# Four tiles to a round in an attention layer: a Trainium2 kernel of four graph layers

## The chip, the cores and the metric

The kernel runs on one NeuronCore of a Trainium2 chip. Five engines work side by side, each through its own list of instructions in order: PE (TensorE, matrix products; the loading of its weights is listed apart as PEld), DVE (VectorE), ACT (ScalarE), POOL (GpSimd) and SP (which only issues DMAs). An instruction waits until what it depends on is done, and whatever is behind it on its engine waits with it. Products land in PSUM, which ACT and DVE can read and write; everything else lies in SBUF. The metric is the device time of one execution in microseconds (us). The kernel before took 625.76 us, the median of 3 runs (624.59 to 626.89).

## What is computed

The input is `x` (4096 x 64) and a 0/1 adjacency matrix `adj` (4096 x 4096, one entry in about a thousand set). Four layers are applied, each to the normalised rows of `x`, each added to `x`. Layer 0 is the one that matters here:

```python
h = jnp.maximum(_layernorm(x, axis=-1), 0.0)
# in layer 0:
h = lorentz_linear(x, W, b, scale)
q = lorentz_linear(h, Wq, bq, scale_q)
k = lorentz_linear(h, Wk, bk, scale_k)
qm = jnp.concatenate([-q[:, :1], q[:, 1:]], axis=-1)
att = 2.0 + 2.0 * (qm @ k.T)
att = jax.nn.sigmoid(att / att_scale + att_bias)
att = adj * att
support = att @ h
inner = -support[:, :1] ** 2 + jnp.sum(support[:, 1:] ** 2, axis=-1, keepdims=True)
denorm = jnp.sqrt(jnp.clip(jnp.abs(-inner), 1e-08, None))
return support / denorm
```

So a full 4096 x 4096 matrix of scores is formed, passed through a sigmoid, masked by `adj` and multiplied by `h`, all in float32. Layers 1 to 3 use `adj` again: as weights by rank of the neighbour, as a plain sum, and as a mean over neighbours.

## The kernel before

**Tiles.** The output rows are cut into 8 blocks of 512 (`IB`), the neighbours into 16 groups of 256 (`NG` groups of `CG` = 2 times 128). A tile is one block by one group: 128 partitions x 1024 numbers. Layer 0 has 8 x 16 = 128 tiles. For each tile

- PE forms the scores: four records of `scores` (line 908), a product with 64 rows that uses the upper and the lower half of the array at once;
- ACT takes the sigmoid, from PSUM back into the same PSUM (`sigmoids`, line 914);
- DVE multiplies by the mask and writes `att` in SBUF (`masked`, line 927), which sets the PSUM buffer free;
- PE gathers: `gather` (line 935) adds the tile's product with `fb` (the rows h) to the block's sum, with 64 columns, the left and the right half of the array at once.

**Rounds.** In the main loop of layer 0 (from line 1024) PE is given the scores of a round of tiles, then the gathers of the round before, then the next scores. The sizes of the rounds are written out: 3, 3, 3, 3, 2, 2 for a block's 16 tiles. Three PSUM buffers hold scores (two of pool `pp`, one of `spare`), taken in turn, so tile n needs what tile n-3 had. Four buffers (`ATTS`) hold `att`.

**Beside each tile** the loop issues one load of a mask (POOL, line 176: float32 in HBM, 8-bit in SBUF), on ten tiles of sixteen one check that half a tile of `adj` is 0 or 1 (`check`, line 351: SP loads 256 KB into one of three buffers, DVE reads them), and one step of the jobs in hand (`step`). A job is the end of a block (`rows0`): PE transposes its sum (line 229, in `turned`), POOL, ACT and DVE normalise it and make layer 1's features `h` from it, which are written into `fa` and split by `split` into two half-precision parts in `s2a`. Six tiles after a block's first gather, the queries of the next block are transposed on PE from `fa` (line 846) and laid out by ACT (line 856).

**The first block** is done otherwise. Its tiles, the first two of the next block and the whole preparation of h, q and k go as parts with a duration each into `Listing`: `plan` takes at each step the part that can begin first, with places (PSUM and `att` buffers) that a part takes and another frees; `run` tries 2,500 random shifts of the parts' ranks and emits the best plan found. While it runs, `spare` does not exist yet, so two PSUM buffers hold scores.

**Memory.** `fa` holds first the queries, then the features of layer 1, then those of later layers. When layer 0 is done its pools are closed, and `s2b` and the buffers `ckw` of the later, larger checks take their memory.

Of the kernel before, what the change touches and what calls it, by code (L numbers as in the profile page):

```python
# [11 lines left out]
F32 = mybir.dt.float32  # L12
BF16 = mybir.dt.bfloat16
FP8 = mybir.dt.float8e4
FP16 = mybir.dt.float16
# [33 lines left out]
def kernel(  # L49
# [84 lines left out]
    def model(general):  # L134
# [10 lines left out]
        ROWS = ((16, 16), (0, 16))  # L145
        main = pool("main", 1)
        x_sb = main.tile([P, NT, D], F32, name="x_sb" + sfx)
        fa = main.tile([P, NT, D], F32, name="fa" + sfx)
        rdegs = main.tile([P, NT], F32, name="rdegs" + sfx)

        def rows_in(gr):
# [27 lines left out]

        EARLY = 4  # L180
        CHECKED = 3
        ATTS = 2 if general else 4
        parts = pool("parts", 1)
        s2a = parts.tile([P, NT, 2, D], FP16, name="s2a" + sfx)
        epi = pool("epi", 1)
        pm = pool("pm", 1, space=PSUM)
        mp0 = pool("mask_a", 1, side="right")
# [75 lines left out]

        def norm(rows, h, tag, table, up=UP):

            xr = x_sb[:, rows, :]
            st = small("st", tag)
            nc.vector.tensor_reduce(st, xr, AX.X, ALU.add)
            nc.vector.tensor_scalar(st, st, -1.0 / D, None, ALU.mult)  # L269
            yield  # L270
            xc = rows_tile("xc", tag)
            nc.gpsimd.tensor_tensor(xc, xr, bc(st, CI), ALU.add)  # L272
            yield
            sq = rows_tile("sq", tag)
            nc.scalar.activation(sq, xc, AF.Square)
            yield
            va = small("va", tag)
            nc.vector.tensor_reduce(va, sq, AX.X, ALU.add)
            if table:
                yield  # L280
                rs = small("rs", tag)
                nc.scalar.activation(
                    rs, va, AF.Sqrt, bias=eps if up == 1.0 else eps_up, scale=1.0 / D / up / up
                )
                yield
                nc.vector.reciprocal(rs, rs)
            else:
                nc.vector.tensor_scalar(va, va, 1.0 / D / up / up, EPS / up / up, ALU.mult, ALU.add)
                rs = rsqrt(va, tag)
                yield  # L290
                yield
                yield
            nc.vector.scalar_tensor_tensor(h, xc, 0.0, bc(rs, CI), ALU.max, ALU.mult)
            yield

        jobs = deque()

# [96 lines left out]
        class Listing:  # L394
# [3 lines left out]

            HOP, TRIALS = 0.15, 2500

            def __init__(self):
                self.parts = []

            def add(self, engine, us, emit, *after, takes=(), frees=None, at=0.0):
                part = SimpleNamespace(
                    engine=engine, us=us, emit=emit, after=after, takes=takes, frees=frees, at=at,
                    n=len(self.parts), then=[], place=None,
                )  # L410
                for q in after:
                    q.then.append(part)
                self.parts.append(part)
                return part

            def plan(self, names, lead):

                busy, places = {}, dict.fromkeys(names, 0.0)
                at = [part.at for part in self.parts]
                open_ = [len(part.after) for part in self.parts]  # L420
                able = [part for part in self.parts if not part.after]
                where, order, last = {}, [], 0.0
                while able:
                    best = None
                    for part in able:
                        t, place = max(at[part.n], busy.get(part.engine, 0.0)), None
                        if part.takes:
                            free = [(places[n], n) for n in part.takes if places[n] is not None]
                            if not free:
                                continue  # L430
# [8 lines left out]
                    end = busy[part.engine] = t + part.us  # L439
                    last = max(last, end)  # L440
# [46 lines left out]
        def before0(todo, gr, bias):  # L487
# [284 lines left out]
            def qk_rows(u, j, engine):  # L772
                def emit(_):
# [4 lines left out]
                    to = v.kr[:, of(u), :] if j else fa[:, rows(u), :]  # L778
# [7 lines left out]
            def qk_times(u, j):  # L786
                def emit(_):
                    part = slice(u * 2 * HR, (u + 1) * 2 * HR)
                    to = v.kr[:, of(u), :] if j else fa[:, rows(u), :]
# [52 lines left out]
        def queries_turned(ib, pt):  # L842

            for k in range(CI // 2):
                c = ib * CI + 2 * k
                nc.tensor.transpose(
                    pt[:, k, :], fa[:, c : c + 2, :].rearrange("p c d -> p (c d)"), ident
                )

        def queries_laid(ib, pt):  # L850
# [18 lines left out]
        def rows0(ib, asb):  # L869
# [20 lines left out]
            yield  # L890
            yield
            yield
            h = fa[:, rows, :]
            yield from norm(rows, h, tag, False)
            yield from split(h, s2a, rows)
            ready.setdefault(1, set()).add(ib)

# [12 lines left out]
                )  # L910
            return ps

        def sigmoids(ps):
            nc.scalar.activation(ps, ps, AF.Sigmoid, bias=att_c, scale=att_a)  # L914

        def masked(ib, g, ps):

            att = work.tile(
                [P, CG, IB], F32, tag="att", name=f"att_{ib}_{g}{sfx}", bufs=ATTS
            )  # L920
            mask = masks[ib][:, g * CG : (g + 1) * CG, :]
            if general:
                at = load(stream0, ib, g, "at0")
                nc.vector.tensor_tensor(att, ps, at, ALU.mult)
                nc.vector.tensor_scalar(mask, at, 0.0, None, ALU.not_equal, saturate=False)
            else:
                nc.vector.tensor_tensor(att, ps, mask, ALU.mult)  # L927
            return att

        def gather(acc, lhs, g, rhs, at):  # L930

# [8 lines left out]
        def first_rows_and_block():  # L940
# [33 lines left out]
            for n, (ib, g) in enumerate(todo[: NG + 2]):  # L974
# [6 lines left out]
                def emit_scores(_, tile=tile):  # L981
                    tile.ps = scores(tile.ib, tile.g)

                def emit_masked(_, tile=tile):
                    tile.att = masked(tile.ib, tile.g, tile.ps)
                    v.att.append((tile.ib, tile.g, tile.att))

                def emit_gather(_, tile=tile):
                    gather(v.acc, fb, tile.g, tile.att, v.at)
                    v.at += 1  # L990

                sc = add(
                    "PE", 1.0, emit_scores, ktd[u], asked[ib], *(scored if begun else ()),
                    takes=("pp0", "pp1"),
                )
                sg = add("ACT", 1.2, lambda _, tile=tile: sigmoids(tile.ps), sc)
                mu = add(
                    "DVE", 1.25, emit_masked, sg, *(spread if begun else ()), frees=sc,
                    takes=slots,
                )  # L1000
                if begun:
                    continue
                scored.append(sc)
                spread.append(mu)
                add("PE", 1.0, emit_gather, mu, hw[u], room, frees=mu)
            listing.run(("pm", "pa", "ps", "pp0", "pp1", *slots))
            return v.acc, v.att[-2:]

        with tc.manual_schedule():
            acc, late = first_rows_and_block()  # L1010
# [13 lines left out]

            sizes = [2] * 8 if general else [3, 3, 3, 3, 2, 2]
            sizes = sizes[:-1] + (NIB - 2) * sizes + [0]
            k, done = NG + 2, NG
            for size in sizes:  # L1030
                now = []
                for ib, g in todo[k : k + size]:
                    ps = scores(ib, g)
                    sigmoids(ps)
                    now.append((ib, g, masked(ib, g, ps)))
                    load_masks(1)
                    k += 1
                    if k % 8 in (0, 2, 4, 5, 7):
# [18 lines left out]


        s2b = None
        if not general:  # L1060
            s2b = pool("parts_b", 1).tile([P, NT, 2, D], FP16, name="s2b")
            more[:] = pool("ck2", 1), 4
        evac = pool("evac", 1)
        l1 = ExitStack()
# [475 lines left out]
```

## Time and profile before

The profiled execution took 628.15 us by the clock outside, of which its span is 626.3 us. What follows is of that span.

| stage | from, us | to, us | length, us |
|---|---|---|---|
| preparation | 0 | 59.23 | 59.2 |
| rest of the first block, in the planned order | 59.23 | 94.85 | 35.6 |
| main loop of layer 0 | 94.85 | 317.06 | 222.2 |
| layers 1 to 3 | 317.06 | 626.3 | 309.2 |

| a tile of layer 0 | engine | mean ns |
|---|---|---|
| sigmoid, line 914 | ACT | 1175 |
| mask, line 927 | DVE | 1220 |
| check of half a tile, line 351 | DVE | 722 |
| issue of a mask's load, line 176 | POOL | 559 |

The first table comes from the start times of PE's instructions, the second from the groups by line. PE's own records overlap one another (each matmul starts before the one before it has drained), so its pace is read from the distance of starts, not from durations.

### The profile page before, as it was taken

To read this page: it belongs to the slowest core of one execution; us is meant where nothing else is said; L and a number is where in the kernel's file an instruction comes from. 1 tells how busy PE (TensorE), PEld (TensorE's weight loads), DVE (VectorE), ACT (ScalarE), POOL (GpSimd) and SP (SyncE) were. 2 spreads that over 40 slices of the span, in tenths; PEclk is the share of its full clock that TensorE was granted. 3 is DMA by queue.
4 is the path that set the end of the run, shared out by engine and by line. 5 is a ranking of instruction groups with operands and counts; after the bars stand their busy time and mean duration, and the time that the engine had idled before them with its cause. 6 is when DMAs were issued, how large, how long until landed. Compare 5 with 4: busy or idle time off the path is not lost.

```text
span 626.3 us, 9053 instructions
## 1 busy us (share of the span) xinstructions
PE 573.7 (92%) x3012; PEld 232.0 (37%) x3012; DVE 483.8 (77%) x951; ACT 337.1 (54%) x541; POOL 225.4 (36%) x459
## 2 busy tenths in 40 slices
PE   0776999999999999999998999999999999998995
PEld 0653223333333333333343344343443544444542
DVE  5768567998888888888968767768666669988853
ACT  1467567666667676666624676767665014431220
POOL 7423301565656564733336300100000314543152
PEclk9996999999999999999998999999998999999998
DMA  8991924699999898982276342333434375558921
GB/s 138 141 103 12 104 23 77 99 153 140 160 144 158 141 151 144 141 154 84 85 255 194 125 135 100 105 131 102 130 107 134 131 255 189 173 181 291 326 101 40
DMA packets 43880, 87.03 MB, mean 139 GB/s; under 512 B 5232, under 2 KB 22256, under 8 KB 43824
## 3 DMA queue, kind: packets, MB, share of 16 engines
q1 hardware_dynamic: 24672, 68.53, 33.3%
q0 software_dynamic: 18720, 17.57, 30.3%
q8 instruction: 25, 0.41, 0.3%
q10 hardware_dynamic: 432, 0.26, 0.2%
q14 instruction: 31, 0.25, 0.1%
HBM read 135.63 MB, written 1.05 MB: 218 GB/s over the span
## 4 chain that ended last, share of the span: by engine, by line
PE 67%; DVE 14%; DMA 6%; POOL 4%; issue 4%; ACT 4%; SPq 0%; DVEq 0%; POOLq 0%; ACTq 0%
PE ps L908 15%; PE acc L935 14%; PE acc L1293 10%; PE acc L1223 9%; PE cnt L1185 9%; DVE ckw L351 4%; PE cnt L1195 3%; DVE att L927 3%; DMA ckw<-adjt_dram 3%; DMA mask<-adjt_dram 2%; ACT ps L914 2%; PE pt L229 1%; DMA x_sb<-x_dram 1%; PE ps_h L615 1%; PE pr L1099 1%
## 5 line engine op out<-in xcount | busy, mean ns | idle before, releaser
L914 ACT ACTIVATE ps<-ps,att_c,att_a 128x1024 f32<-128x1024 f32 x128 | 146.9, 1175 | 82.7 <-PE ps L908 82.6
L927 DVE TENSOR_TENSOR att<-ps,mask 128x1024 f32<-128x1024 f32 x128 | 155.1, 1220 | 39.0 <-ACT ps L914 38.2
L908 PE MATMUL ps<-qt,kt 64*128 64x512 f32 x512 | 133.6, 630 | 5.2 <-DVE att L927 4.3
L351 DVE SCALAR_TENSOR_TENSOR ckw<-ckw 128x1024 f32<-128x1024 f32 x93 | 119.5, 1298 | 8.0 <-DMA ckw<-adjt_dram 8.0
L935 PE MATMUL acc<-att,fb 128*64 128x512 f32 x512 | 123.1, 607 | 0.7 <-DVE att L927 0.7
L1211 ACT ACTIVATE w<-cnt 128x512 int16<-128x512 f32 x176 | 93.1, 597 | 49.1 <-PE cnt L1195 48.8
L1209 DVE TENSOR_SCALAR w<-cnt 128x512 int16<-128x512 f32 x80 | 53.7, 688 | 38.0 <-PE cnt L1195 37.2
L176 POOL DMA_DIRECT2D mask<-adjt_dram x128 | 70.1, 559 | 20.4 <-DMA mask<-adjt_dram 18.6
L908 PEld LDWEIGHTS ps<-qt,kt 64*128 64x128 f32 x512 | 44.0, 187 | 87.5 <-DVE att L927 41.1
L1185 PE MATMUL cnt<-mask,after 128*128 128x512 fp8e4 x256 | 67.6, 385 | 4.7 <-DVE w L1209 4.3
L1223 PE MATMUL acc<-w,s2a 128*128 128x512 bf16 x256 | 67.8, 387 | 0.1
L935 PEld LDWEIGHTS acc<-att,fb 128*64 128x64 f32 x512 | 31.8, 136 | 81.1 <-issue 76.6
L272 POOL TENSOR_TENSOR xc<-x_sb,st 128x256 f32<-128x256 f32 x24 | 19.0, 793 | 110.0 <-DVE st L269 69.1
L1293 PE MATMUL acc<-mask,s2a 128*128 128x512 fp8e4 x256 | 57.8, 379 | 0.0
L1293 PE MATMUL acc<-mask,s2b 128*128 128x512 fp8e4 x256 | 57.7, 379 | 0.0
L351 DVE SCALAR_TENSOR_TENSOR ck<-ck 128x512 f32<-128x512 f32 x70 | 50.5, 722 | 0.0
L258 POOL TENSOR_TENSOR rs_a<-rs_y 128x4 f32<-128x4 f32 x48 | 17.3, 360 | 89.4 <-DVE rs_y L254 81.2
L1185 PEld LDWEIGHTS <-after 128*128 128x128 bf16 x256 | 25.1, 100 | 34.5 <-issue 7.7
L1293 PEld LDWEIGHTS <-s2b 128*128 128x128 f16 x256 | 25.0, 98 | 27.6 <-issue 0.8
L1293 PEld LDWEIGHTS <-s2a 128*128 128x128 f16 x256 | 24.7, 98 | 27.3
L1223 PEld LDWEIGHTS <-s2a 128*128 128x128 f16 x256 | 20.0, 98 | 30.7 <-issue 15.6
L213 ACT ACTIVATE asb<-acc,level 128x512 f32<-128x512 f32 x23 | 15.4, 692 | 28.3 <-PE acc L1293 28.3
(192 smaller groups left out, 531.9 us busy)
## 6 DMA issues: line engine op xcount, KB each, us to landing
ckw<-adjt_dram SPq DMA_DIRECT2D x93, 512.0 KB, 4.1
ck<-adjt_dram SPq DMA_DIRECT2D x70, 256.0 KB, 5.8
mask<-adjt_dram POOLq DMA_DIRECT2D x128, 128.0 KB, 9.4
x_sb<-x_dram SPq DMA_DIRECT2D x4, 256.0 KB, 8.2
out_dram<-y POOLq DMA_DIRECT2D x6, 128.0 KB, 2.2
w_sb<-wts_dram SPq DMA_DIRECT2D x2, 80.0 KB, 7.9
vec<-vecs_dram ACTq DMA_DIRECT2D x1, 130.5 KB, 6.1
out_dram<-y SPq DMA_DIRECT2D x1, 128.0 KB, 1.9
```

Of the source, the lines that this page charges most:

```text
L176: nc.gpsimd.dma_start(out=masks[ib][:, g * CG : (g + 1) * CG, :], in_=adjt[ib, g])
L272: nc.gpsimd.tensor_tensor(xc, xr, bc(st, CI), ALU.add)
L351: nc.vector.scalar_tensor_tensor(at, at, 0.0, at, ALU.not_equal, ALU.not_equal, accum_out=odd[:, k : k + 1])
L908: nc.tensor.matmul(ps[:, c, :], kt[half, g, :], qts[ib][half, :], start=True, stop=True)
L914: nc.scalar.activation(ps, ps, AF.Sigmoid, bias=att_c, scale=att_a)
L927: nc.vector.tensor_tensor(att, ps, mask, ALU.mult)
L935: nc.tensor.matmul(acc[c * D : (c + 1) * D, :], lhs[:, t, :], rhs[:, c, :], start=(at == 0), stop=(at == NG - 1), skip_group_check=True,)
L1185: nc.tensor.matmul(cnt, after, masks[ib][:, t, :], start=True, stop=True, skip_group_check=True)
L1209: nc.vector.tensor_scalar(w, cnt, 0.0, None, ALU.max)
L1211: nc.scalar.activation(w, cnt, AF.Relu)
L1223: nc.tensor.matmul(accs[ib], both(s2a, t), w, start=(t == NT - 1), stop=False, skip_group_check=True,)
L1293: nc.tensor.matmul(acc, both(s2, t), masks[ib][:, t, :], start=(t == 0), stop=(t == NT - 1), skip_group_check=True,)
```

## The change

- **Rounds of four.** The main loop's rounds become 4, 4, 3, 3 for the rest of the second block and 4, 4, 4, 4 for every later one. There are still three PSUM buffers.
- **The first of a round is masked in SBUF.** In a round of four, the first tile's sigmoid is written by ACT into its `att` buffer in SBUF, and DVE multiplies there in place. Its PSUM buffer is free after the sigmoid. In the planned first block this holds for all 18 tiles.
- **Six `att` buffers** in place of four.
- **Queries share memory with `s2a`.** `q_sb` is the memory of `s2a` read as float32. `fa` is made only after layer 0, and the job's `h` of layer 1 stays in `xc`.
- **The plan counts changes of mode.** Scores and gathers get a `form`; `plan` adds `TURN` = 0.12 us where an engine's form changes, and scores and gathers count 0.88 us in place of 1.0. A score's PSUM place is freed by the sigmoid, and the `att` place is taken by the sigmoid.

```diff
-        fa = main.tile([P, NT, D], F32, name="fa" + sfx)
...
-        ATTS = 2 if general else 4
+        ATTS = 2 if general else 6
         parts = pool("parts", 1)
         s2a = parts.tile([P, NT, 2, D], FP16, name="s2a" + sfx)
+        q_sb = s2a.rearrange("p t k d -> p t (k d)").bitcast(F32)
...
+            h = xc if h is None else h
             nc.vector.scalar_tensor_tensor(h, xc, 0.0, bc(rs, CI), ALU.max, ALU.mult)
...
-            HOP, TRIALS = 0.15, 2500
+            HOP, TURN, TRIALS = 0.15, 0.12, 2500
...
-                        t, place = max(at[part.n], busy.get(part.engine, 0.0)), None
+                        free_at = busy.get(part.engine, 0.0)
+                        if forms.get(part.engine) != part.form:
+                            free_at += self.TURN
+                        t, place = max(at[part.n], free_at), None
...
-            h = fa[:, rows, :]
-            yield from norm(rows, h, tag, False)
+            h = yield from norm(rows, None, tag, False)
...
-        def sigmoids(ps):
-            nc.scalar.activation(ps, ps, AF.Sigmoid, bias=att_c, scale=att_a)
+        def sigmoids(ps, to=None):
+            to = ps if to is None else to
+            nc.scalar.activation(to, ps, AF.Sigmoid, bias=att_c, scale=att_a)
+            return to
...
-                nc.vector.tensor_tensor(att, ps, mask, ALU.mult)
+                nc.vector.tensor_tensor(att, frm, mask, ALU.mult)
...
                 sc = add(
-                    "PE", 1.0, emit_scores, ktd[u], asked[ib], *(scored if begun else ()),
-                    takes=("pp0", "pp1"),
+                    "PE", 0.88, emit_scores, ktd[u], asked[ib], *(scored if begun else ()),
+                    takes=("pp0", "pp1"), form="scores",
                 )
-                sg = add("ACT", 1.2, lambda _, tile=tile: sigmoids(tile.ps), sc)
-                mu = add(
-                    "DVE", 1.25, emit_masked, sg, *(spread if begun else ()), frees=sc,
+                sg = add(
+                    "ACT", 1.2, emit_sigmoids, sc, *(spread if begun else ()), frees=sc,
                     takes=slots,
                 )
+                mu = add("DVE", 1.25, emit_masked, sg)
...
-            sizes = [2] * 8 if general else [3, 3, 3, 3, 2, 2]
-            sizes = sizes[:-1] + (NIB - 2) * sizes + [0]
+            sizes = [2] * 8 if general else [4] * 4
+            first = [2] * 7 if general else [4, 4, 3, 3]
+            sizes = first + (NIB - 2) * sizes + [0]
...
-                    sigmoids(ps)
-                    now.append((ib, g, masked(ib, g, ps)))
+                    if size == 4 and not now:
+                        att = frm = sigmoids(ps, att_tile(ib, g))
+                    else:
+                        frm, att = sigmoids(ps), att_tile(ib, g)
+                    masked(ib, g, frm, att)
+                    now.append((ib, g, att))
...
+        parts_b = pool("parts_b", 1)
+        fa = parts_b.tile([P, NT, D], F32, name="fa" + sfx)
         if not general:
-            s2b = pool("parts_b", 1).tile([P, NT, 2, D], FP16, name="s2b")
+            s2b = parts_b.tile([P, NT, 2, D], FP16, name="s2b")
             more[:] = pool("ck2", 1), 4
```

More of the change, by code (lines that the diff above doesn't have):

```diff
@@ L292, in norm @@
                 yield
+            h = xc if h is None else h
             nc.vector.scalar_tensor_tensor(h, xc, 0.0, bc(rs, CI), ALU.max, ALU.mult)
             yield
+            return h
         jobs = deque()
@@ L394, in model, with add @@
         class Listing:
-            HOP, TRIALS = 0.15, 2500
+            HOP, TURN, TRIALS = 0.15, 0.12, 2500
             def __init__(self):
                 self.parts = []
-            def add(self, engine, us, emit, *after, takes=(), frees=None, at=0.0):
+            def add(self, engine, us, emit, *after, takes=(), frees=None, at=0.0, form=None):
                 part = SimpleNamespace(
                     engine=engine, us=us, emit=emit, after=after, takes=takes, frees=frees, at=at,
-                    n=len(self.parts), then=[], place=None,
+                    form=form, n=len(self.parts), then=[], place=None,
                 )
@@ L416, in plan @@
             def plan(self, names, lead):
-                busy, places = {}, dict.fromkeys(names, 0.0)
+                busy, forms, places = {}, {}, dict.fromkeys(names, 0.0)
                 at = [part.at for part in self.parts]
@@ L439, in plan @@
                     end = busy[part.engine] = t + part.us
+                    forms[part.engine] = part.form
                     last = max(last, end)
@@ L777, in emit @@
                     r3 = v.rrq[:, part].rearrange("p (s k j) -> p s k j", s=2, j=2)[:, :, :, j]
-                    to = v.kr[:, of(u), :] if j else fa[:, rows(u), :]
+                    to = v.kr[:, of(u), :] if j else q_sb[:, rows(u), :]
                     engine.tensor_tensor(
@@ L788, in emit @@
                     part = slice(u * 2 * HR, (u + 1) * 2 * HR)
-                    to = v.kr[:, of(u), :] if j else fa[:, rows(u), :]
+                    to = v.kr[:, of(u), :] if j else q_sb[:, rows(u), :]
                     nc.scalar.mul(
@@ L846, in queries_turned @@
                 nc.tensor.transpose(
-                    pt[:, k, :], fa[:, c : c + 2, :].rearrange("p c d -> p (c d)"), ident
+                    pt[:, k, :], q_sb[:, c : c + 2, :].rearrange("p c d -> p (c d)"), ident
                 )
@@ L911, in scores, with att_tile, masked @@
             return ps
-        def sigmoids(ps):
-            nc.scalar.activation(ps, ps, AF.Sigmoid, bias=att_c, scale=att_a)
-        def masked(ib, g, ps):
-            att = work.tile(
+        def att_tile(ib, g):
+            return work.tile(
                 [P, CG, IB], F32, tag="att", name=f"att_{ib}_{g}{sfx}", bufs=ATTS
             )
+        def sigmoids(ps, to=None):
+            to = ps if to is None else to
+            nc.scalar.activation(to, ps, AF.Sigmoid, bias=att_c, scale=att_a)
+            return to
+        def masked(ib, g, frm, att):
             mask = masks[ib][:, g * CG : (g + 1) * CG, :]
@@ L923, in masked @@
                 at = load(stream0, ib, g, "at0")
-                nc.vector.tensor_tensor(att, ps, at, ALU.mult)
+                nc.vector.tensor_tensor(att, frm, at, ALU.mult)
                 nc.vector.tensor_scalar(mask, at, 0.0, None, ALU.not_equal, saturate=False)
             else:
-                nc.vector.tensor_tensor(att, ps, mask, ALU.mult)
-            return att
+                nc.vector.tensor_tensor(att, frm, mask, ALU.mult)
         def gather(acc, lhs, g, rhs, at):
@@ L982, in emit_scores, with emit_sigmoids @@
                     tile.ps = scores(tile.ib, tile.g)
+                def emit_sigmoids(_, tile=tile):
+                    tile.att = sigmoids(tile.ps, att_tile(tile.ib, tile.g))
                 def emit_masked(_, tile=tile):
-                    tile.att = masked(tile.ib, tile.g, tile.ps)
-                    v.att.append((tile.ib, tile.g, tile.att))
+                    masked(tile.ib, tile.g, tile.att, tile.att)
+                    if tile.ib != last:
+                        v.att.append((tile.ib, tile.g, tile.att))
                 def emit_gather(_, tile=tile):
@@ L1003, in first_rows_and_block @@
                 scored.append(sc)
-                spread.append(mu)
-                add("PE", 1.0, emit_gather, mu, hw[u], room, frees=mu)
+                spread.append(sg)
+                add("PE", 0.88, emit_gather, mu, hw[u], room, frees=sg, form="gather")
             listing.run(("pm", "pa", "ps", "pp0", "pp1", *slots))
-            return v.acc, v.att[-2:]
+            return v.acc, v.att
         with tc.manual_schedule():
```

## The prediction

> **What bounds the kernel now.** I read the page's chain of waits first, to see which engine sets the end, then the groups for its lines:
>
> ```profile
> PE 67%; DVE 14%; DMA 6%; POOL 4%; issue 4%; ACT 4%; SPq 0%; DVEq 0%; POOLq 0%; ACTq 0%
> ...
> L914 ACT ACTIVATE ps<-ps,att_c,att_a 128x1024 f32<-128x1024 f32 x128 | 146.9, 1175 | 82.7 <-PE ps L908 82.6
> L927 DVE TENSOR_TENSOR att<-ps,mask 128x1024 f32<-128x1024 f32 x128 | 155.1, 1220 | 39.0 <-ACT ps L914 38.2
> L908 PE MATMUL ps<-qt,kt 64*128 64x512 f32 x512 | 133.6, 630 | 5.2 <-DVE att L927 4.3
> ```
>
> PE holds 67% of the chain, and ACT's idle time before its sigmoids (82.7 us) is waiting for PE's scores. So layer 0 is PE's. How close the others are is seen in a table of stretches cut at one block's length (columns: stretch, length, then busy time of PE, PEld, DVE, ACT, POOL, granted clock, DMA share, GB/s):
>
> ```profile
> 163.12:195.08 31.96, 31.33 (x135) 10.00 (x134) 27.94 (x51) 21.39 (x25) 18.61 (x47) 1.00 1.00 152
> 195.08:227.05 31.97, 31.34 (x136) 10.01 (x135) 27.95 (x51) 21.40 (x25) 18.61 (x47) 1.00 0.98 148
> 259.26:291.23 31.97, 31.34 (x136) 10.01 (x135) 27.94 (x51) 21.40 (x25) 14.11 (x38) 1.00 0.71 131
> ```
>
> A block takes 31.97 us, with PE busy nearly throughout at full clock. DVE works 27.94, so a block can be shortened by at most 4.0 before DVE is the bound. The third row has a DMA share of 0.71 against 1.00 and the same length: DMA does not set the pace. Last, PE's timeline over part of a block (start, duration, instruction; x4 is one tile):
>
> ```profile
> 186.14 2.85 PE L908 MATMUL ps<-qt,kt 64*128 64x512 f32 x12
> 188.91 1.94 PE L935 MATMUL acc<-att,fb 128*64 128x512 f32 x8
> 190.78 2.04 PE L908 MATMUL ps<-qt,kt 64*128 64x512 f32 x8
> 193.44 1.13 PE L908 MATMUL ps<-qt,kt 64*128 64x512 f32 x4 [0.61 <-DVE att L927]
> 194.50 0.66 PE L229 MATMUL pt<-ident,asb 128*128 128x128 f32 x4
> 195.08 2.79 PE L935 MATMUL acc<-att,fb 128*64 128x512 f32 x12
> 197.81 2.85 PE L908 MATMUL ps<-qt,kt 64*128 64x512 f32 x12
> ...
> 203.31 3.13 PE L908 MATMUL ps<-qt,kt 64*128 64x512 f32 x12
> 206.38 2.79 PE L935 MATMUL acc<-att,fb 128*64 128x512 f32 x12
> 209.10 1.13 PE L908 MATMUL ps<-qt,kt 64*128 64x512 f32 x4
> 210.16 0.44 PE L846 MATMUL pq<-ident,fa 128*128 128x128 f32 x2
> 210.53 1.13 PE L908 MATMUL ps<-qt,kt 64*128 64x512 f32 x4
> ```
>
> Take distances of starts. Scores of one tile: 210.16 - 209.10 = 1.06; of three: 188.91 - 186.14 = 2.77. So 0.86 for a tile and **0.20 for the turn** into scores. Gathers of two tiles: 1.87, of three: 2.73, so 0.86 a tile and **0.15 for the turn** into gathers. A pair of turns costs 0.35, whatever the round's size. A job's transposes cost 0.58 (194.50 to 195.08), the queries' 0.37, and since those split a round, another 0.20. Then a block is 32 x 0.86 = 27.52, six pairs = 2.10, 0.58, 0.57: 30.77. The missing 1.2 are two waits for a PSUM buffer, whose mask DVE finished late: the third tile at 193.44 comes 0.94 late (3.72 to 194.50 where 2.77 would do), that of the round at 203.31 0.29.
>
> **Main loop, rounds of four.** Four pairs of turns in place of six: -0.70 a block. The job's transposes now come after the third tile of a round instead of at a round's end, so they split it: +0.20. A block's work is 27.52 + 1.40 + 0.78 + 0.57 = 30.27, if PE never waits. Over the loop: 222 tile passes (110 scores, 112 gathers) x 0.86 = 190.9; 28 pairs = 9.8; seven transposes at 0.78 = 5.5; six queries at 0.57 = 3.4; sum 209.6, against 222.2 now. **At most 12.6 us**: 13 pairs = 4.55, less 1.4 for split rounds, and 9.5 of waits.
>
> Do the waits go? The fourth tile needs the first one's PSUM. PE gets there 0.20 + 3 x 0.86 = 2.78 after the round's start. ACT begins 1.17 after it and takes 1.18: free at 2.4, so covered by 0.4. Masked from PSUM, it would be free at 2.38 + 1.22 + 0.05 = 3.65, a wait of 0.9 in every round. Tiles two to four of the next round wait for DVE's masks. I walked one block with DVE's order kept: masks 1.15 apart, a check 0.61, the job's pieces 0.4 to 1.2. The tightest are the third tile of the second round (mask finished 0.35 before PE needs it) and of the fourth (0.31). DVE is then idle 2.3 of 30.27. Next: the queries. Transposed inside the fourth round, they are laid out by ACT behind that round's last sigmoid and ready about 0.6 before the next block's scores, where now there are several us; without that cover PE would wait for the excess. Margins of 0.3 are about one collision on DVE (below), so I leave 0.4 a block, **2.5 in all. Gain: 10.1.**
>
> **ACT writes SBUF.** No sigmoid does so yet. A page of the Trainium skill speaks against it: "ScalarE: Activation LUTs", on the profile stage ("Step-by-step: what each stage is for"), calls ACT's way to PSUM faster than that to SBUF. The nearest row:
>
> ```profile
> L758 ACT COPY tq<-ps_q x4: 995/1012/1013, 37.5 to 47.4; 128x1024 f32<-128x1024 f32 x4
> ```
>
> That is PSUM to SBUF in 1.01, of the same size. The sigmoid (1.18, PSUM to PSUM) also reads two pointer operands, which the same page ("What ACT_TABLE_LOAD costs") prices at 0.093 each: 1.01 + 0.19 = 1.20. So SBUF costs between 0 and 0.03 more by the row; the rule gives no number, and up to 0.4 would be hidden. I take 0.
>
> **DVE with two inputs in SBUF.** This is the rule that matters. "SBUF — State Buffer" ("Who interferes with whom") says that a DVE instruction with both inputs in SBUF contends with a POOL instruction that reads SBUF, and that the later one waits for the whole other. The mask products have one input in PSUM today. The checks have both in SBUF (two rows of the timeline):
>
> ```profile
> 308.77 1.06 DVE L351 SCALAR_TENSOR_TENSOR ck<-ck 128x512 f32<-128x512 f32 x1
> 309.36 1.05 POOL L888 TENSOR_TENSOR x_sb<-x_sb,sup 128x256 f32<-128x256 f32 x1
> ```
>
> Their shortest are 0.67 and 0.72; so the trace agrees, +0.38. But the checks' mean, 0.722, is only 0.04 above their median 0.681. By the mean, scaled to the longer product, 26 products cost 26 x 0.07 = 2 us of DVE over the loop; by the rule at its worst, a full POOL instruction (1.05) each time, 27, or 4.2 a block. I take the row: it lies in the 0.4 a block. A product may also gain a little without PSUM; taken as 0.
>
> **Six buffers.** The third tile's product needs a buffer that the gathers of the round before free. These begin right after the round's scores; DVE gets there after that in each round I walked. No cost; with four buffers DVE would wait for the next gathers.
>
> **First block.** From 59.23 to 94.85 PE does 32 passes one by one: 16 turns into scores and 14 into gathers, 3.2 + 2.1 = 5.3 us. Two PSUM buffers, freed by the sigmoid, allow pairs (a third tile would wait for the first sigmoid until 2.4, PE is there at 1.92). Eight pairs of turns cost 2.8: gain 2.5. Bounds: 4 (threes, and an earlier third tile at 59.23, which waits 0.35 for a mask) and -1 (another plan may order the preparation worse; the plan's durations are not the chip's). **I take 2.5.**
>
> **Memory and later layers.** Queries in `s2a` and `h` in `xc` add no instruction; `xc` is overwritten eight tiles after its last reader. `fa` under `s2b` moves `ckw` up by 8 KB, off `fb`. Its first load is issued at 316.41, when the last gather ends, and DVE waits for it until 320.08. It may now start earlier, as its memory was last read by scores: 0 to 1.5, **I take 0.4.** Everything later only moves forward.
>
> **Sum.** 10.1 + 2.5 + 0.4 = 13.0. Span 626.3 - 13.0 = 613.3; own time 628.15 - 13.0 = 615.2. The median lies 2.4 below the profiled time and moves alike: 625.76 - 13.0 = **612.8 us**.
>
> **Rivals.**
>
> - *DVE becomes the bound through POOL (slower).* Place: the first product of each round, beside POOL's normalising chain. Price: 1.05 each is 4.2 a block; DVE then needs 27.94 + 4.2 = 32.1, and what DVE waits for POOL's late results (it takes them in order) adds some 0.5. At 32.6 the loop's 6.9 blocks lose 4.5; with the first block's 18 products delayed too, its gain is gone: 630. It decides from 2.3 a block on, DVE's idle time. For it: DVE is the tightest engine. Against: the checks' mean.
> - *The waits stay, or DMA holds the pace.* A third PSUM buffer still late costs 9.5 as now: only 3.1 + 2.5 gained, 620. Likewise DMA: a block reads 16 x 0.524 + 10 x 0.262 = 11.0 MB, 344 GB/s now, 363 needed. Were 344 the ceiling, blocks would keep 31.97 until the masks are in at 278, giving 621. Against: from 20 to 40 us mask loads write 106 GB/s, a quarter of what they read, so about 420 is possible. But checks land only 0.3 to 2 us before use at times.
> - *The new plan brings nothing.* First block unchanged: 10.5 gained, 615.3.
>
> **How the numbers follow.** Forecast 0.60, plan without gain 0.10, waits or DMA 0.22, DVE bound 0.08. About 0.5%, 3.1 us, tells a change from none. Faster: 0.60 + 0.10 + 0.15 = 0.85; same 0.07 (the rest of the second rival); slower 0.08. Best end: no waits (12.6), 3.5 and 1 give 608.6, rounded down; the other end is the second rival, 621. Range 608 to 621.
>
> **What would show it.** Starts of scores in fours 3.64 apart to the next gathers; a block of 30.3 to 30.8; hardly any idle of PE before line 908; the first block's gathers in twos; sigmoids to `att` at 1.2. I am wrong if blocks stay near 32 with PE waiting for DVE, if first products take 1.5 and more, if scores of a new block wait for `qt`, or if checks wait for DMA.

## The result, and the profile after

The changed kernel took 616.55 us (median of 6 runs, 615.8 to 618.12), the kernel before 626.83 on the same chip (6 runs, 624.59 to 628.02): ratio 0.9858, 95% interval 0.9836 to 0.988. That is **8.9 us less (7.5 to 10.3)**, where 13.0 was forecast. The spans of the two profiled executions, 626.3 and 614.1, differ by 12.2. That is more than the ratio gives, because the profile of before was taken in an execution above its median (628.15) and that of after in the fastest of its six (615.8). The quotient of the two medians would be 0.9836, or 10.3 us, at the far end of the interval; what follows uses the ratio.

From the page of the kernel after, first the engine shares of the chain that ended last, then groups (line, engine, operation, shapes, count; busy us and mean ns of one; idle us before, with what ended most of it):

```profile
PE 70%; DVE 12%; POOL 5%; DMA 4%; issue 4%; ACT 4%; SPq 0%; DVEq 0%; POOLq 0%; ACTq 0%
...
L916 PE MATMUL ps<-qt,kt 64*128 64x512 f32 x512 | 127.7, 622 | 5.4 <-DVE att L940 5.0
...
L940 DVE TENSOR_TENSOR att<-ps,mask 128x1024 f32<-128x1024 f32 x84 | 101.5, 1220 | 7.6 <-ACT ps L929 6.8
L929 ACT ACTIVATE ps<-ps,att_c,att_a 128x1024 f32<-128x1024 f32 x84 | 95.7, 1174 | 12.2 <-PE ps L916 11.8
L929 ACT ACTIVATE att<-ps,att_c,att_a 128x1024 f32<-128x1024 f32 x44 | 52.5, 1204 | 56.2 <-PE ps L916 53.2
...
L940 DVE TENSOR_TENSOR att<-att,mask 128x1024 f32<-128x1024 f32 x44 | 56.1, 1291 | 17.1 <-ACT att L929 16.6
...
L356 DVE SCALAR_TENSOR_TENSOR ck<-ck 128x512 f32<-128x512 f32 x70 | 52.0, 744 | 0.3 <-DMA ck<-adjt_dram 0.3
...
L260 POOL TENSOR_TENSOR rs_a<-rs_y 128x4 f32<-128x4 f32 x48 | 17.4, 363 | 83.3 <-DVE rs_y L256 75.1
```

Scores are now line 916, gathers 947, the sigmoid 929, the product 940. PE's share of the chain rose from 67 to 70%; DVE's fell from 14 to 12. Two new groups of 44 show what became of the first tiles: the sigmoid that writes SBUF takes 1.204 us, 0.03 more than the other, and the product with both inputs in SBUF 1.291, 0.07 more. The checks waited for DMA 0.3 us in all, so DMA didn't hold the pace. But the idle time of PE before the scores is 5.4 us, hardly changed from 5.2: waits are left, and the rest of this document is largely about them.

The steady part of the main loop, in blocks (length, then busy time of PE, PEld, DVE, ACT, POOL, clock, DMA share, GB/s), and PE's timeline over the second of them:

```profile
130.21:160.44 30.23, 30.23 (x136) 10.44 (x134) 28.48 (x50) 21.02 (x24) 18.14 (x42) 1.00 1.00 154
160.44:190.76 30.32, 30.32 (x137) 10.36 (x135) 28.46 (x48) 21.24 (x25) 20.92 (x46) 1.00 1.02 157
190.76:221.60 30.84, 30.84 (x136) 10.27 (x134) 29.00 (x49) 21.28 (x25) 21.51 (x48) 1.00 1.03 155
```

```profile
160.44 3.65 PE L947 MATMUL acc<-att,fb 128*64 128x512 f32 x16
164.03 3.70 PE L916 MATMUL ps<-qt,kt 64*128 64x512 f32 x16
167.66 3.65 PE L947 MATMUL acc<-att,fb 128*64 128x512 f32 x16
171.25 2.85 PE L916 MATMUL ps<-qt,kt 64*128 64x512 f32 x12
174.02 0.44 PE L855 MATMUL pq<-ident,s2a 128*128 128x128 f32 x2
174.39 1.13 PE L916 MATMUL ps<-qt,kt 64*128 64x512 f32 x4
```

Scores of four tiles take 3.63 from start to start (164.03 to 167.66) and gathers 3.59: four times 0.86 and a turn of 0.20 or 0.15. A block is 30.2 to 30.8 us where it was 31.97. So the forecast's steady block (30.27, 30.7 with its waits) is what the chip does. The shortfall must lie elsewhere, and a table by stage says where. "Waits" is what PE spends in the main loop beyond 0.86 a tile pass, the turns and the transposes; the columns before and after hold for one profiled execution each.

| us | before | predicted | after |
|---|---|---|---|
| first block's end (first scores of the main loop) | 94.85 | 92.35 | 89.22 |
| main loop | 222.2 | 212.1 | 217.3 |
| of it waits | 9.45 | 2.5 | 7.9 |
| layers 1 to 3 | 309.3 | 308.9 | 307.6 |

The loop gained 4.9 instead of 10.1, all of the shortfall in its waits (the same sum over the rounds as they ran is 209.4, forecast 209.6); the first block gained more than forecast. Place by place, from the distances of PE's starts, the waits are 4.5 us up to 130.2, before the steady blocks; 2.1 near 247; 0.7 at the end, where the last gathers wait for the last masks; and 0.6 elsewhere, in two pieces of 0.2 and 0.4. All other starts fit the unit costs to 0.1 us in all.

### The profile page after: what moved, and what is told of

It is laid out like the page before. It is cut to its first block, busy times and chain, and to the rows that moved or that the text cites. A ratio compares the mean times of both kernels' runs of the same rounds, so it can differ in the third digit from the quotient of the medians.

```text
span 614.1 us, 9025 instructions
## 1 busy us (share of the span) xinstructions
PE 563.7 (92%) x3012; PEld 234.0 (38%) x3012; DVE 487.1 (79%) x951; ACT 335.5 (55%) x541; POOL 239.0 (39%) x459
## 3 DMA queue, kind: packets, MB, share of 16 engines
q0 software_dynamic: 18720, 17.57, 30.6%
HBM read 135.63 MB, written 1.05 MB: 223 GB/s over the span
## 4 chain that ended last, share of the span: by engine, by line
PE 70%; DVE 12%; POOL 5%; DMA 4%; issue 4%; ACT 4%; SPq 0%; DVEq 0%; POOLq 0%; ACTq 0%
PE ps L916 17%; PE acc L947 16%; PE acc L1318 10%; PE acc L1248 9%; PE cnt L1210 9%; DVE ckw L356 4%; PE cnt L1220 3%; DMA ckw<-adjt_dram 3%; DVE att L940 2%; PE ps_h L624 1%; PE pt L231 1%; PE pr L1124 1%; DMA vec<-vecs_dram 1%; POOL y L1428 1%; DVE ck L356 1%
## 5 line engine op out<-in xcount | busy, mean ns | idle before, releaser
L916 PE MATMUL ps<-qt,kt 64*128 64x512 f32 x512 | 127.7, 622 | 5.4 <-DVE att L940 5.0
L947 PE MATMUL acc<-att,fb 128*64 128x512 f32 x512 | 117.6, 599 | 0.2 <-DVE att L940 0.2
L940 DVE TENSOR_TENSOR att<-ps,mask 128x1024 f32<-128x1024 f32 x84 | 101.5, 1220 | 7.6 <-ACT ps L929 6.8
L929 ACT ACTIVATE ps<-ps,att_c,att_a 128x1024 f32<-128x1024 f32 x84 | 95.7, 1174 | 12.2 <-PE ps L916 11.8
L929 ACT ACTIVATE att<-ps,att_c,att_a 128x1024 f32<-128x1024 f32 x44 | 52.5, 1204 | 56.2 <-PE ps L916 53.2
L940 DVE TENSOR_TENSOR att<-att,mask 128x1024 f32<-128x1024 f32 x44 | 56.1, 1291 | 17.1 <-ACT att L929 16.6
L947 PEld LDWEIGHTS acc<-att,fb 128*64 128x64 f32 x512 | 33.6, 136 | 79.4 <-issue 75.4
L356 DVE SCALAR_TENSOR_TENSOR ck<-ck 128x512 f32<-128x512 f32 x70 | 52.0, 744 | 0.3 <-DMA ck<-adjt_dram 0.3
L1318 PEld LDWEIGHTS <-s2a 128*128 128x128 f16 x256 | 24.6, 98 | 27.3
```

What stands on the lines that cost most here:

```text
L356: nc.vector.scalar_tensor_tensor(at, at, 0.0, at, ALU.not_equal, ALU.not_equal, accum_out=odd[:, k : k + 1])
L916: nc.tensor.matmul(ps[:, c, :], kt[half, g, :], qts[ib][half, :], start=True, stop=True)
L929: nc.scalar.activation(to, ps, AF.Sigmoid, bias=att_c, scale=att_a)
L940: nc.vector.tensor_tensor(att, frm, mask, ALU.mult)
L947: nc.tensor.matmul(acc[c * D : (c + 1) * D, :], lhs[:, t, :], rhs[:, c, :], start=(at == 0), stop=(at == NG - 1), skip_group_check=True,)
L1318: nc.tensor.matmul(acc, both(s2, t), masks[ib][:, t, :], start=(t == 0), stop=(t == NT - 1), skip_group_check=True,)
```

## The experiments

In each the edit is made to the changed kernel, and the ratio is to the kernel before, with its 95% interval. My theory at the start: the parts add; the main loop lost its gain in the second block and at one stall; the SBUF mask of the first tile is what allows rounds of four.

**One part alone.** The rounds of four with the old plan's parts, and the new plan with the old rounds (six buffers in both):

```diff
 rounds alone
-sg = add("ACT", 1.2, emit_sigmoids, sc, *(spread if begun else ()), frees=sc, takes=slots)
-mu = add("DVE", 1.25, emit_masked, sg)
+sg = add("ACT", 1.2, emit_sigmoids, sc)
+mu = add("DVE", 1.25, emit_masked, sg, *(spread if begun else ()), frees=sc, takes=slots)
...
 plan alone
-sizes = [2] * 8 if general else [4] * 4
-first = [2] * 7 if general else [4, 4, 3, 3]
+sizes = [2] * 8 if general else [3, 3, 3, 3, 2, 2]
+first = sizes[:-1]
```

(In "rounds alone" PE's parts are also 1.0 long without a form, and the first block's sigmoid stays in PSUM, as before.)

> The first block is planned and masked as before (sigmoid in PSUM, a PSUM place freed by the mask, durations of 1.0, no form), six buffers; the main loop is that of the change. If the two parts are independent, the main loop takes 217.3 us as in the changed kernel and the first block 35.6 as before (its end at 94.9): span 614.1 + 5.6 = 619.7, ratio to before near 0.990. Rival: the waits of the second block (4.5 us in the changed kernel) come from how the new plan leaves DVE and ACT at the hand-over; then they are gone here and the span is 615 to 617.

> The first block and the six buffers are those of the change; the main loop has its old rounds of 3, 3, 3, 3, 2, 2, all masked from PSUM. If independent, the first block ends at 89.2 as in the changed kernel and the main loop takes about 222 us: span 626.3 - 5.6 - 0 to 1.6 = 619 to 621. Rival: six buffers alone already shorten the old loop (DVE no longer waits for a buffer); then the loop is under 220.

Rounds alone: 621.03, 0.9904 (0.987 to 0.9939). Plan alone: 622.18, 0.993 (0.9905 to 0.9956). Their loops are 217.4 and 222.2, their first blocks end at 93.62 and 90.85. So the two add: each stage follows its own part and doesn't notice the other. And since plan alone has six buffers and a loop of 222.19 against 222.21, six buffers by themselves bring nothing to the loop.

**The second block.** Its rounds are 4, 4, 3, 3. Three views of the kernel after, in the part where PE stands longest. ACT (start, duration, instruction, idle before and its releaser):

```profile
111.47 1.18 ACT L929 ACTIVATE ps<-ps,att_c,att_a 128x1024 f32<-128x1024 f32 x1 [3.36 <-PE ps L916]
112.57 1.51 ACT L865 COPY qt<-pq 64x256 f32<-64x256 f32 x4
114.11 1.18 ACT L929 ACTIVATE ps<-ps,att_c,att_a 128x1024 f32<-128x1024 f32 x1
```

DVE, and then PE:

```profile
115.32 1.23 DVE L940 TENSOR_TENSOR att<-ps,mask 128x1024 f32<-128x1024 f32 x1 [1.42 <-ACT ps L929]
...
117.07 0.22 DVE L837 TENSOR_SCALAR tri<-ident 128x128 f32<-128x128 f32 x1
...
118.69 1.22 DVE L940 TENSOR_TENSOR att<-ps,mask 128x1024 f32<-128x1024 f32 x1
```

```profile
115.79 1.99 PE L916 MATMUL ps<-qt,kt 64*128 64x512 f32 x8
119.96 1.99 PE L916 MATMUL ps<-qt,kt 64*128 64x512 f32 x8 [2.18 <-DVE att L940]
```

The copies of the next queries (1.51) stand between the first two sigmoids of a round: in a block of 4, 4, 3, 3 the query transposes fall at a round's end, and the copies, one step later, into the next round, where the steady block has them behind a round's last sigmoid. The mask of the second tile is late with its sigmoid. Then DVE builds the constants for the counting of later layers (from 117.07 to 118.69), in front of the mask that PE waits for from 117.7 on. Each cause was taken away alone, then both:

```diff
-first = [2] * 7 if general else [4, 4, 3, 3]
+first = [2] * 7 if general else [2, 4, 4, 4]
...
-push(count_constants(), 1)
...
+for _ in count_constants():
+    pass
 acc, late = first_rows_and_block()
```

> The changed kernel with rounds 2, 4, 4, 4 in place of 4, 4, 3, 3 for the rest of the second block, so that every later round begins at a multiple of four tiles. Theory: in the changed kernel the queries' copies stand on ACT before the second sigmoid of a round there (at 112.6), which makes two masks late; aligned, they come after the last sigmoid, as in the later blocks. The waits of that stretch fall from 4.5 us to about 1.7 (the constants' 1.6 us on DVE stay): loop 214.5, span 611.3. Rival: the constants for the counts on DVE (at 117 to 118.6) are the whole cause; then the waits stay at 3.5 to 4.5 and the span within 1 us of 614.

> The changed kernel with the constants for the later counts (about 1.6 us of small DVE instructions and 0.6 of POOL) made before the first block's plan, where DVE waits for x, instead of in the second block. Theory (queries' copies on ACT are most of the cause): the wait at 115.8 falls from 2.4 by at most 1.6, the following one by some of 1.2; span 612 to 613. Rival (the constants are the whole cause): 3.5 us and more go, span under 611.

> Both edits: rounds 2, 4, 4, 4 in the second block and the constants made before the first block. Theory: the second block then runs like the later ones, 30.3 us a block with waits of under 1 us: loop 213, span 610, ratio to before near 0.976. Rival (a later stage takes back what the loop gains, or waits move to the third block): span 612 and more.

| | loop | waits | median | ratio |
|---|---|---|---|---|
| after | 217.28 | 7.9 | 616.55 | 0.9858 (0.9836 to 0.988) |
| short round first | 215.51 | 5.9 | 615.64 | 0.9828 (0.9789 to 0.9868) |
| constants early | 215.71 | 6.3 | 616.09 | 0.9835 (0.9795 to 0.9874) |
| both | 213.95 | 4.35 | 616.44 | 0.9826 (0.9806 to 0.9846) |

The loop shrinks by 1.8, 1.6 and 3.3: in the loop both causes are real and they add. PE's timeline of the kernel with both, at the same place:

```profile
110.89 3.70 PE L916 MATMUL ps<-qt,kt 64*128 64x512 f32 x16
114.53 3.65 PE L947 MATMUL acc<-att,fb 128*64 128x512 f32 x16
118.11 3.70 PE L916 MATMUL ps<-qt,kt 64*128 64x512 f32 x16
```

No wait is left here. In the times, though, the gain isn't visible: all intervals overlap, and none of these versions is shown to beat the change. The loop repeats within 0.2 us; the stages around it do not (below). Nor are the constants free in their new place. DVE's first reduction of `x` stands behind them: it starts at 9.84 in the kernel with the constants early alone, at 7.08 in the kernel after. The four kernels with early constants end the first block at 90.6 to 92.4, mean 91.2, against 89.9 for the seven that otherwise share its plan. So about 1.2 of the 1.6 us may only have moved, though the two groups overlap a little.

**Is the SBUF mask needed?** All sigmoids of the main loop into PSUM, rounds of four kept:

```diff
-if size == 4 and not now:
+if False:
```

> The changed kernel without the first tile of a round in SBUF: in the main loop every sigmoid stays in PSUM and every PSUM buffer is freed by the mask, still in rounds of four. My prediction said a wait of 0.9 us in every round of four then: 26 x 0.87 = 22.6 us, part of it taking the place of the waits that are there now (7.7): loop 232 to 240, span 629 to 637, slower than before. Rival (a fourth tile finds its buffer free anyway): within 3 us of 614.

635.51, ratio 1.014 (1.0111 to 1.0168), loop 236.1. PE's timeline:

```profile
170.79 2.85 PE L916 MATMUL ps<-qt,kt 64*128 64x512 f32 x12
174.46 1.13 PE L916 MATMUL ps<-qt,kt 64*128 64x512 f32 x4 [0.82 <-DVE att L940]
```

The fourth tile comes 3.67 after the first where 2.77 would do: 0.9 us late, as forecast for a product from PSUM. So it is in the two rounds of a block that no transposes split. In the other two the transposes stand ahead of the fourth tile and use up part of the wait: 0.3 is left with a job's, 0.5 with the queries'. Rounds of four without the detour through SBUF would have made the kernel slower than it was.

**And if every tile takes that detour?** This was the rule that spoke against the change, at four times the dose:

```diff
-if size == 4 and not now:
+if not general:
```

> The changed kernel with every sigmoid of the main loop written to SBUF and every product with both inputs in SBUF. By the row (the product took 1.29 with both inputs in SBUF, 1.22 with one) DVE works 84 x 0.07 = 5.9 us more over the loop, 0.9 a block of its 2.3 idle, and PE's scores wait for sigmoids alone: loop within 3 us of 217.3, rather shorter, span 612 to 615. By the rule that each such product can wait for a whole POOL instruction (1.05), DVE has up to 13 us a block more and is the bound: span above 640.

647.64, ratio 1.0328 (1.031 to 1.0346), loop 249.7, waits 40. My theory fell. Its page, the chain and two groups:

```profile
PE 43%; DVE 19%; POOL 17%; DMA 8%; issue 7%; ACT 4%; DVEq 0%; POOLq 0%; ACTq 0%
...
L940 DVE TENSOR_TENSOR att<-att,mask 128x1024 f32<-128x1024 f32 x128 | 161.8, 1287 | 17.3 <-ACT att L929 16.8
...
L260 POOL TENSOR_TENSOR rs_a<-rs_y 128x4 f32<-128x4 f32 x48 | 31.4, 654 | 76.3 <-DVE rs_y L256 68.5
```

The product is no slower than in the change (1.287), so DVE's own sum did not rise beyond what the row said. POOL pays: its small operation of line 260 takes 0.654 instead of 0.363, and POOL is 17% of the chain instead of 5. Side by side, DVE's timeline and POOL's:

```profile
162.44 2.36 DVE L940 TENSOR_TENSOR att<-att,mask 128x1024 f32<-128x1024 f32 x2
...
169.20 0.43 DVE L297 SCALAR_TENSOR_TENSOR xc<-xc,rs_y 128x256 f32<-128x256 f32 x1 [2.05 <-POOL rs_y L263]
```

```profile
162.61 1.11 POOL L260 TENSOR_TENSOR rs_a<-rs_y 128x4 f32<-128x4 f32 x1 [3.21 <-DVE rs_y L256]
163.80 1.05 POOL L261 TENSOR_TENSOR rs_a<-rs_a,va 128x4 f32<-128x4 f32 x1
...
168.13 0.20 POOL L260 TENSOR_TENSOR rs_a<-rs_y 128x4 f32<-128x4 f32 x1
```

While the two products run, a POOL operation that takes 0.20 us elsewhere starts and lasts until the product beside it ends: 1.11, 1.05. From 167.2 on DVE does nothing that reads two SBUF operands, and the same operations take 0.20. This is the lock that the Trainium skill describes ("SBUF — State Buffer", "Who interferes with whom"), and at 162.61 the whole wait is on POOL. Then DVE, which takes its work in order, waits 2.05 for POOL's result, with masks behind it. The waits between 130 and 330 us (engine and line, what for; us in total, times, longest):

```profile
ACT sq L278 <- POOL xc L275: 27.6, 5, 7.5
ACT att L929 <- PE acc L947: 20.9, 12, 3.2
ACT sq L888 <- POOL sup L239: 18.6, 6, 5.1
...
DVE st L271 <- POOL x_sb L897: 15.0, 5, 3.1
...
DVE xc L297 <- POOL rs_y L263: 12.3, 6, 2.3
```

One line fits a rival: ACT waits 20.9 us for gathers, which is a lack of buffers, since a buffer is now held from the sigmoid on. So rounds of three were run with every tile in SBUF (the sizes of "plan alone" and the condition above):

> Every sigmoid of the main loop to SBUF, as in the run before, but in the old rounds of 3, 3, 3, 3, 2, 2: a tile's buffer is then that of two rounds ago, whose gathers PE has done before the tile is scored, so ACT never waits for a buffer. It is to be compared with the old rounds in PSUM (loop 222.2). Theory: products with two inputs in SBUF hold up POOL's chains of short instructions, and DVE and ACT then wait in order for POOL's results; this stays here in full: loop 230 or more, POOL's line 260 at 0.6 us a piece in the mean. Rival: what made the loop 249.7 long were the waits for buffers (ACT waited 20.9 us for gathers); then the loop is at most 222, as PE's scores no longer wait for masks.

One execution, so without an interval: 648.44, loop 250.6. Between 130 and 320 us ACT has no wait for gathers any more, and yet:

```profile
ACT sq L278 <- POOL xc L275: 28.2, 5, 7.4
ACT sq L888 <- POOL sup L239: 16.8, 6, 3.6
DVE st L271 <- POOL x_sb L897: 16.3, 5, 3.3
...
DVE xc L297 <- POOL rs_y L263: 10.2, 5, 2.0
```

The buffer rival falls; what remains is POOL. That POOL's delays make the whole length is read from these waits; no run moved POOL's work away. With plan alone (222.2, the same rounds and buffers, products from PSUM) it differs only in where the sigmoids go: 28 us for that. In rounds of four, with no, one or all four tiles of a round masked in SBUF the loop is 236.1, 217.3 and 249.7.

POOL pays at one tile of four too. In line 260 alone it hardly shows; in the next lines of the same chain it does. One line between 100 and 300 us, in the kernel before and in the kernel after (there 262):

```profile
L260 POOL TENSOR_SCALAR rs_a<-rs_a 128x4 f32<-128x4 f32 x36 | 6.9, 192 | 3.2
```

```profile
L262 POOL TENSOR_SCALAR rs_a<-rs_a 128x4 f32<-128x4 f32 x38 | 14.8, 390 | 3.4
```

All 156 operations of this chain in the main loop (lines 258 to 261 before, 260 to 263 after) take 35.7 us before, 39.1 in rounds of four from PSUM, 50.3 in the change and 81.1 with every tile in SBUF. In the change the steady blocks don't show it (30.2 to 30.8 us).

**The turn in the plan.** The plan's price for a mode change set to nothing:

```diff
-HOP, TURN, TRIALS = 0.15, 0.12, 2500
+HOP, TURN, TRIALS = 0.15, 0.0, 2500
```

> The changed kernel with TURN = 0 in the plan, nothing else. The first block gained 5.6 us where I counted 2.5 for its turns; two of its tiles are now scored before 59 us. Theory: the freeing by the sigmoid gives the early tiles (2.1 us) and stays; the turns go back to one tile each: first block 3 us longer than in the changed kernel, span 617. Rival: freeing by the sigmoid alone makes the plan run in pairs; then the span is within 1 us of 614.

617.07, ratio 0.985 (0.9812 to 0.9888). The first block ends at 89.36, not 89.22; from the first gather on it takes 30.6 us instead of 30.0. Counting mode changes is worth about 0.6 us. From there on PE's gathers come in 6 runs in the change, in 10 here and in 14 before: some pairs form by themselves once PSUM is freed by the sigmoid, and the price makes more. So most of the first block's gain comes from the plan's other edits; the freeing by the sigmoid, the shorter durations and the six buffers were not tried apart.

**The change once more,** for what repeats:

> The changed kernel as it is, once more, beside the one above on the same chip. Main loop 217.3 within 0.3 us. The stretch before it ended at 89.2 in its profile and at 88.6 to 92.4 in the kernels that share its first block, and the rest took 306.1 to 309.7 in kernels that share all of it: both vary by some 3 us with no edit. So the gain of the first block, 5.6 by the two profiles, should come out nearer to 4, the span at 614 to 617, the ratio to before at 0.983 to 0.987. Rival: the first block gains 5.6 and the span is 614 again.

617.39, ratio 0.9857 (0.9827 to 0.9887). Its loop is 217.34 (217.28 before), but its first block ends at 90.67, 1.45 later with identical code. The seven kernels that share this plan end it between 88.61 and 90.85, mean 89.9; the two with the old plan at 94.85 and 93.62, mean 94.2. So the first block's gain is **about 4.3 us**, not the 5.6 of the first pair of profiles. The variation lies ahead of the first gather, which starts between 58.6 and 60.9 in the seven. From it to the block's end they take 30.0 to 30.1, the old plan 33.8 and 33.1: some 3.5 of the 4.3 stand clear of the variation. Layers 1 to 3 lie between 306.1 and 309.7 in all fourteen profiles; no difference of 2 us there can be given to a part of the change.

**Can the remaining splits of rounds go?** The change splits two rounds a block, for the job's and for the queries' transposes. Both moved to where a round ends, on top of the short round and the early constants:

```diff
 rows of a job
+yield
 yield
 yield
 pt = turned(asb, None, tag)
...
 queries
-for _ in range(6):
+for _ in range(3):
     yield
 pt = pm.tile([P, CI, P], F32, tag="pr", name=f"pq_{ib}{sfx}")
 queries_turned(ib, pt)
-yield
+for _ in range(4):
+    yield
 queries_laid(ib, pt)
```

> Rounds 2, 4, 4, 4 in the second block, the constants early, and the two transposes that split a round moved to a round's end: the job's one tile later, the queries' three tiles earlier (their copies by ACT stay where they were). By the turns: 7 x 0.20 + 6 x 0.20 = 2.6 us less than the 213.95 of the kernel with the first two edits: loop 211.3; with the first block and the rest as usual, a ratio to before near 0.975. Rival: the job's copy now stands on ACT between a round's first two sigmoids, DVE is late by as much, and the wait for a mask takes back the 1.4 us: loop 212.5 to 214.

616.34, ratio 0.9845 (0.9815 to 0.9876), loop 217.2 and waits 10.0: the saved turns came back as waits, and more. One wait of the kernel after, then of this one, between 130 and 300 us:

```profile
ACT sq L278 <- POOL xc L275: 2.4, 2, 2.2
```

```profile
ACT sq L278 <- POOL xc L275: 8.7, 5, 2.3
```

One step later, ACT's square of a job stands ahead of a sigmoid before POOL has its operand ready. Only the queries moved, the job as in the change:

> Rounds 2, 4, 4, 4 in the second block, the constants early, and of the two moves of the run before only that of the queries' transposes to a round's end; the job keeps its place. Theory: what cost whole_rounds its 2.6 us was the job's shift by one tile, which put the job's Square on ACT, waiting for POOL, in front of a round's third sigmoid (ACT waited 8.7 us for POOL in its blocks, 2.4 in the changed kernel). Without the shift the loop is 213.95 less 6 x 0.20: 212.7 us, waits about 4.4; ratio to before 0.980 to 0.984. Rival: the queries' move cost as well; then the loop is 214 to 217.

615.33, ratio 0.9845 (0.9822 to 0.9868), loop 215.3, where 213.95 is had without the move. The waits rose from 4.35 to 6.9, 1.6 of it at the stall near 247 and 1.0 between 130 and 222. Both moves cost more than the turns that they save, this one only together with the stall.

## Why the prediction came out as it did

**The bound and the steady block: right.** PE at full clock set the pace, turns cost 0.20 and 0.15, and a steady block fell to 30.2 to 30.8 with PE busy nearly throughout.

**The waits of the main loop: the mis-sized term.** The sum put "0.4 a block, 2.5 in all"; 7.9 were measured, and that is why the loop gained 4.9 instead of 10.1. The walk that gave 0.4 was made over one steady block, and there it holds. What it left out are the places that are not steady:

- The second block, 4.5 us: queries' copies ahead of a sigmoid, and the constants ahead of a mask. Taking both away gave 3.3 back.
- One stall of POOL, 2.1. POOL's timeline in the kernel after:

```profile
241.40 2.75 POOL L175 DMA_DIRECT2D mask<-adjt_dram  x5 [2.08 <-issue]
244.10 0.67 POOL L275 TENSOR_TENSOR xc<-x_sb,st 128x256 f32<-128x256 f32 x1
```

  POOL stands 2.08 us before a mask load, released by nothing that the profile shows. Its centring of the rows (line 275) is late, with it ACT's square, the sigmoids behind that, and PE's scores at 247.6. Before the change POOL stood there too (1.63 at 248.42), but PE lost only 0.24: that block still held waits of its own, and the delay fell into them. The change took that cover away. This chain is read from the trace; no run removed the stall. It comes at the 114th of the 128 mask loads in all fourteen profiles, whatever stands beside it on POOL, so it goes with that load or with the count of loads, not with what is around it.
- The end of the loop, 0.7: the last gathers wait for the last masks. Before, 1.7 were lost there, so this had been in the trace to see.

**The first block: right in sign, too small.** 2.5 was taken for eight pairs of turns; about 4.3 came, a little past the upper bound of 4. The turns went as forecast: 6 runs of gathers in place of 14, and 7 runs of scores in place of 16, are 3.0 us, where 2.8 less some loss was put. What the sum left out is how many tiles are scored before the first gather. PE's timeline in the kernel before and in the kernel after:

```profile
53.01 3.70 PE L908 MATMUL ps<-qt,kt 64*128 64x512 f32 x8 [0.84 <-ACT qt L856]
58.22 0.66 PE L567 MATMUL pt_k<-ident,kr 128*128 128x128 f32 x4 [1.51 <-ACT kr L790]
59.23 1.84 PE L908 MATMUL ps<-qt,kt 64*128 64x512 f32 x4 [0.35 <-DVE att L927]
```

```profile
53.07 4.88 PE L916 MATMUL ps<-qt,kt 64*128 64x512 f32 x12
58.16 1.13 PE L916 MATMUL ps<-qt,kt 64*128 64x512 f32 x4 [0.21 <-ACT att L929]
59.22 1.08 PE L947 MATMUL acc<-att,fb 128*64 128x512 f32 x4
```

Four tiles are scored by 59.22, where the kernel before had two and stood 1.51 us ahead of 58.22. With PSUM freed by the sigmoid, two passes (2 x 0.86 = 1.7) moved there; the new plan also has those last transposes of the keys earlier, at 50.54. This is the sum of one pair of profiles and not tested by itself. The prediction named an earlier third tile only, and only in its bounds. With 1.8 too little here and 5.2 too much in the loop, and without the 0.4 of the later layers, 13.0 becomes 9.2 by the stages; the ratio gives 8.9. That the total came this near is partly luck: the two errors have opposite signs.

**ACT to SBUF at nothing: right in effect.** It costs 0.03, the upper end of the row's bound, and ACT had idle time. **DVE's product, 0.07 by the row and 1.05 by the rule: the row was right** for the change (1.291 against 1.220). But the slower rival rests on a real mechanism. It named DVE as the one that would wait; the runs show POOL waiting, and the others waiting for POOL's results. At one product of four POOL's chain takes 50.3 us in the loop where it took 35.7, which the steady blocks don't show; at four of four it takes 81.1 and the loop is 32 us longer.

**Six buffers at no cost: not contradicted.** Alone they changed nothing. **Later layers, 0.4: not resolved.** The first wide check load is issued 0.64 before the loop's end in the kernel after (305.85 and 306.49) and 0.65 in the one before, so the moved memory let nothing start earlier against the loop's end.

**The other rivals.** DMA: no, 0.3 us of waiting. The plan bringing nothing: no, plan alone gives 0.993. "A third buffer still late": no as a steady wait; but the waits that came in its place ate half of the gain.

**What stays open:** why POOL stands about 2 us at its 114th mask load; why the time up to the first gather varies by 1.5 us and more between executions of the same code; and what one SBUF product a round costs the loop by itself, which none of the runs separates from the rounds of four.

## What to carry to other kernels

Walk the blocks that are not steady (the first after a start, the one with one-time work, the last) as carefully as the steady one: here the steady block came out as worked out, and all but 0.6 us of the waiting lay in the second block, at one stall and at the end. When a change tightens a loop, list the small late events that the old slack absorbed; they come back in full. A contention that a mean of one engine's instructions shows as small can be paid by the other engine: look at both sides, at every line of the other's chain, and at who waits in order for the slower one. When work is moved out of a stage, look for it where it went.

## What the hardware showed that was not expected

- The lock between DVE and POOL falls on the short operations: with every product reading SBUF twice, DVE's product grew by 0.07 (1.220 to 1.287), while POOL's operations of line 260, 0.20 when nothing is beside them, grew to a mean of 0.65. Those shown took up to 1.1 and ended with the product beside them. With one product in four POOL's chain of 156 such operations already takes 50.3 us instead of 35.7, unseen in the time.
- POOL stands before one mask load with nothing in the profile to release it, always the 114th of 128: 1.63 us in the kernel before and with the plan alone, 2.0 to 2.1 in the other kernels, and 1.40 in the one where the job and the queries were both moved.
